# The first pair of images: plain projections ahead of two attentions, position terms by TensorE, and another order of filters and statistics

## The chip, the cores and the metric

The kernel runs on one core of one Trainium2 chip. The metric is the device time of one execution in microseconds, as the median of five runs. A core has TensorE (PE, with its weight load PEld), VectorE (DVE), ScalarE (ACT), GpSimd (POOL) and SyncE (SP). Each engine works through its own list of instructions in order. SP's list holds most loads from HBM, POOL's list most stores, so an instruction of these two that waits also holds the transfers listed behind it.

## The reference

There are 8 images of 512 x 32 x 32 in fp32. Each is normalised over groups of 16 channels, run through one layer, and added to the input:

```python
t = cbs(x, cv1_w, cv1_bn, 0)                 # 1x1 convolution, 512 -> 512, batch norm, silu
ys = [t[:, :C], t[:, C:]]                    # C = 256
for i in range(N):                           # N = 2
    yi = ys[-1]
    z = cbs(yi, m_cv1_w[i], m_cv1_bn[i], 1)  # 3x3 convolution, 256 -> 256
    z = bot_attention(z, m_qkv_w[i], m_rw[i], m_rh[i])
    z = jax.nn.silu(bn_eval(conv2d(z, m_cv2_w[i], 0), m_cv2_bn[i]))
    ys.append(yi + z)
return cbs(jnp.concatenate(ys, axis=1), cv2_w, cv2_bn, 0)
```

The attention has 4 heads of 64 channels over the 1024 pixels of an image. q, k and v are one 1x1 convolution, 256 to 768. The position term r = rw + rh is added to k; it is the same for all images and has one value for each block i.

## The kernel before

**Pairs.** The images go in four pairs, (0,1) to (6,7). Within a pair, block 0 and block 1 follow each other: a 3x3 convolution of both images, then the projection and attention of the first image, then those of the second. While an attention runs, hooks issue the normalisation and cv1 of the next pair and the transformation of filters, and what they don't finish comes between the two attentions. The two attentions of block 0 are called the first and the second attention here.

**The 3x3 convolution** goes by Winograd tiles of 4 x 4 outputs. `tiles_in` transforms the input on VectorE (w_ec, w_rows, w_d, w_ab, v_in), `conv3x3` multiplies on TensorE (c_ps, L588) and transforms back on VectorE (c_t, c_e, c_r, c_k). The filters are transformed on the chip in the first pair, by `make_u(n, oc, k, area)`: n is the block, oc the block of 128 output channels, k that of input channels. It takes three steps over the filter's rows, with two ScalarE operations and six VectorE operations in each (u_new, L391 to L398) and three more VectorE operations (L375 to L381) ahead of two of the steps, and stores the result through POOL (L402). Later uses load it again with SP (u). For (0, 0, k) the result stays on the chip, in `first_units`.

**Buffers.** Tiles with the same tag share slots. Tag "u" is a ring of ten slots of 4 KB a partition in which filters, filter results (u_new), cv1's weights and the projections' weights follow one another. Tag "pt" has six slots, for the attention's exponentials, the position terms read back (r_in), and the convolution's tiles. Tag "t" has four slots of 2 KB, tag "acc" two. A new tile waits for the last use of the one whose slot it takes, a store's landing included.

**The projection**, `project_strassen` (L778), computes q, k and v by one level of Strassen: seven products instead of eight, each of two matmuls of 512 columns (L791) and four of 128 (L797), with copies on ScalarE and some 21 additions on VectorE (L817 to L870). Its weights are seven sums of blocks of the qkv weights, made by `make_sq` with four operations on VectorE (L212 to L215) and stores, and loaded in four pieces (sq). VectorE makes sums of z for it (t_z, `first_sum`, L775).

**The position terms** are made by `make_r` on POOL: a copy, four additions of 128 x 512 (L200) and four stores (L204) for each block. `project_strassen` reads them back (r_in, L813) and adds them to k (kr, L817). For block 0 `make_r(0, ...)` is issued in the start-up; for block 1 `make_r(1, load_r(1))` is issued after the projection of the second image; its load is issued by SP at 279.20 us of the trace.

**The start-up** normalises image 0 in two halves of 256 channels (`group_norm_part`, statistics on VectorE, or on ScalarE with `by_act`), with gmat, a matrix that POOL makes by two selections (L334, L338), to sum over groups. Image 1 (x_second) takes its statistics from ScalarE. Filters (0, 1, k) are made first and stored, (0, 0, k) after them. `make_sq(0, ...)` comes after the convolution's tiles, with the qkv weights in the padded tiles Y2 (the profile's ypad). `keep_y` stores y0 and y1.

**The order** on each engine comes from a list scheduler, with `tc.issue_after` fixing some instructions behind others. Between the two attentions TensorE does: half of cv1 of an image of the next pair, the first image's last head sums (s_ps, L952), the second image's projection, the first image's second 1x1 convolution (m_ps, L1132), and the rest of cv1. In the direct mode of pair 0, cv1 is plain products of 512 columns (L471).

## Time and profile before

| | us |
|---|---|
| median of five runs | 2366.21 |
| lowest, highest | 2361.94, 2370.42 |
| profiled execution | 2360.92 |
| its span in the trace | 2359.3 |
| TensorE busy | 2227.8 (94%) |
| VectorE busy | 1767.1 (75%) |
| ScalarE busy | 1084.2 (46%) |
| POOL busy | 216.3 (9%) |

The granted TensorE clock was 0.985 of full speed over the span. The stages of pair 0, by events in the trace:

| us | event on TensorE |
|---|---|
| 15.88 | cv1 of image 0 starts |
| 54.75 to 82.42 | cv1 of image 1 |
| 82.42 to 136.16 | 3x3 convolution of both images |
| 136.16 to 160.06 | projection of image 0 |
| 163.55 to 228.45 | first attention, first to last product with v |
| 309.47 | first product with v of the second attention |

Busy time of each engine in these stretches, where a stretch of 69.00 us with PE 60.53 means that TensorE had something in work for 60.53 of them (the lines leave out a column each for the number of instructions):

| stretch | PE | DVE | ACT | POOL |
|---|---|---|---|---|
| 0 to 40 | 19.58 | 26.14 | 15.63 | 22.22 |
| 40 to 82 | 41.06 | 39.03 | 28.69 | 17.01 |
| 82 to 110 | 12.20 | 25.56 | 3.48 | 3.36 |
| 110 to 136 | 25.14 | 24.25 | 5.16 | 0.77 |
| 136 to 160 | 20.73 | 15.75 | 10.54 | 0.54 |
| 160 to 229 | 60.53 | 58.91 | 41.62 | 6.65 |
| 229 to 252 | 16.90 | 11.96 | 5.33 | 6.48 |
| 252 to 310 | 46.12 | 33.83 | 21.00 | 16.34 |

In the lists of waits below, a row names the engine and the instruction that waited, after the arrow the instruction that released it, then the total in us, the number of waits, and the longest. In rows in order of time, the columns are the start, the duration, the engine, the line, the operation, the tiles written and read, and in brackets the idle time before and its releaser. One fp32 matmul instruction appears as two records.

### The profile page before, as it was taken

What the parts mean: (1) busy time and instruction counts of PE and PEld (TensorE: products, weight loads), DVE (VectorE), ACT (ScalarE), POOL (GpSimd) and SP (SyncE); (2) the same over time, 40 slices, a digit from 0 to 9 for tenths busy, and PEclk for the clock granted to TensorE, in tenths of its full rate; (3) what the DMA queues carried; (4) which work ended last, traced back from release to release, by engine and by line L of the source; (5) the groups of instructions that cost most, each with busy time, mean ns of one, the idle gap of its engine ahead of it and who ended that gap; (6) DMA issues with size and microseconds to landing.
All of it is one profiled execution on the core that took longest, in us unless ns stands there. A gap on an engine that the chain in (4) does not pass through costs nothing.

```text
span 2359.3 us, 40593 instructions
## 1 busy us (share of the span) xinstructions
PE 2227.8 (94%) x16378; PEld 1083.3 (46%) x16378; DVE 1767.1 (75%) x2669; ACT 1084.2 (46%) x1321; POOL 216.3 (9%) x423
## 2 busy tenths in 40 slices
PE   6798878999999999999999999999999999999997
PEld 2463423734447343744346444473344734373433
DVE  7987587877857878986775868887794777787652
ACT  5245444355323666355522565635532355336532
POOL 5101210000021000000012000000002100000003
PEclk9899989999999999999999999999999999999999
DMA  9632623621257051523147323351225711161105
GB/s 330 228 121 73 229 81 119 243 87 55 59 152 256 25 174 47 181 95 104 33 114 232 108 87 116 95 195 60 65 66 149 247 34 59 50 203 38 55 19 140
DMA packets 133251, 284.58 MB, mean 121 GB/s; under 512 B 34272, under 2 KB 60368, under 8 KB 132032
## 3 DMA queue, kind: packets, MB, share of 16 engines
q1 hardware_dynamic: 105712, 198.14, 26.0%
q0 software_dynamic: 27344, 83.77, 11.6%
q8 instruction: 131, 2.15, 0.4%
q14 instruction: 64, 0.52, 0.1%
HBM read 213.83 MB, written 68.03 MB: 119 GB/s over the span
## 4 chain that ended last, share of the span: by engine, by line
PE 53%; DVE 23%; issue 11%; DMA 7%; ACT 3%; POOL 2%; SPq 0%; DVEq 0%; POOLq 0%; ACTq 0%
PE av_ps L935 15%; PE l_ps L901 15%; PE p_ps L791 6%; DMA c_out<-in_x_dram 4%; PE m_ps L1132 4%; PE x_ps L1252 3%; PE ps L471 3%; PE c L1152 2%; PE pv_ps L797 2%; DVE acc L921 2%; DVE c_e L596 1%; ACT pt L905 1%; DVE c_t L595 1%; DVE c_t L594 1%; PE s_ps L952 1%
## 5 line engine op out<-in xcount | busy, mean ns | idle before, releaser
L905 ACT ACTIVATE pt<-l_ps 128x1024 f32<-128x1024 f32 x512 | 495.8, 1023 | 366.2 <-PE l_ps L901 333.5
L921 DVE TENSOR_TENSOR acc<-acc,pt 128x1024 f32<-128x1024 f32 x384 | 469.9, 1224 | 88.2 <-ACT pt L905 65.7
L901 PE MATMUL l_ps<-q,kr 64*64 64x512 f32 x4096 | 493.8, 596 | 29.1 <-ACT pt L905 16.3
L935 PE MATMUL av_ps<-pt,vT 64*64 64x512 f32 x4096 | 488.9, 594 | 10.7 <-DVE z L943 8.5
L901 PEld LDWEIGHTS l_ps<-q,kr 64*64 64x64 f32 x4096 | 157.5, 134 | 304.2 <-issue 246.9
L935 PEld LDWEIGHTS av_ps<-pt,vT 64*64 64x64 f32 x4096 | 154.9, 133 | 286.9 <-issue 238.9
L588 PE MATMUL c_ps<-v_in,u 128*64 128x128 f32 x4320 | 239.5, 273 | 5.4 <-issue 4.5
L588 PEld LDWEIGHTS c_ps<-v_in,u 128*64 128x64 f32 x4320 | 235.8, 137 | 12.6 <-issue 11.5
L791 PE MATMUL p_ps<-t_z,sq 128*128 128x512 f32 x256 | 124.6, 608 | 14.0 <-DVE c_t L595 9.1
L1132 PE MATMUL m_ps<-z,m_sb 128*128 128x512 f32 x256 | 112.5, 592 | 0.0
L593 ACT COPY c_m<-c_ps 128x512 f32<-128x512 f32 x48 | 28.1, 586 | 171.4 <-PE c_ps L588 112.2
L919 DVE TENSOR_TENSOR acc<-pt 128x1024 f32<-128x1024 f32 x64 | 78.0, 1218 | 30.7 <-ACT pt L905 30.7
L791 PE MATMUL p_ps<-z,sq 128*128 128x512 f32 x192 | 91.7, 604 | 9.6 <-ACT z L445 9.6
L445 ACT ACTIVATE t<-m_ps,bh,sh 128x512 f32<-128x512 f32 x64 | 47.0, 776 | 87.5 <-PE m_ps L1132 86.9
L1202 POOL DMA_DIRECT2D c_out<-in_x_dram x56 | 49.7, 960 | 304.0 <-ACT c_out L445 301.0
L1132 PEld LDWEIGHTS m_ps<-z,m_sb 128*128 128x128 f32 x256 | 48.2, 190 | 58.4 <-issue 54.8
L1007 DVE TENSOR_TENSOR z<-z,rs 128x512 f32<-128x512 f32 x64 | 44.0, 687 | 34.4 <-DMA rs<-r_dram 34.2
L791 PEld LDWEIGHTS p_ps<-t_z,sq 128*128 128x128 f32 x256 | 44.9, 193 | 51.7 <-issue 34.3
L506 POOL MEMSET w_rows<- 128x32 f32 x48 | 7.9, 164 | 646.3 <-PE s_ps L952 381.2
L797 PEld LDWEIGHTS pv_ps<-sq,z 128*128 128x128 f32 x384 | 49.0, 191 | 29.1 <-issue 11.7
L943 DVE TENSOR_TENSOR z<-av_ps,z 128x512 f32<-128x512 f32 x64 | 43.9, 686 | 22.0 <-ACT z L942 22.0
L445 ACT ACTIVATE c_out<-cz,bh,sh 128x512 f32<-128x512 f32 x14 | 16.7, 1298 | 91.9 <-DVE cz L1229 91.9
(299 smaller groups left out, 3189.9 us busy)
## 6 DMA issues: line engine op xcount, KB each, us to landing
u<-u SPq DMA_DIRECT2D x135, 512.0 KB
sq<-sq SPq DMA_DIRECT2D x48, 384.0 KB
r_in<-r SPq DMA_DIRECT2D x32, 512.0 KB
rs<-r_dram SPq DMA_DIRECT2D x120, 128.0 KB
x<-in_x_dram SPq DMA_DIRECT2D x28, 512.0 KB
y_in<-y SPq DMA_DIRECT2D x28, 512.0 KB
c_out<-in_x_dram POOLq DMA_DIRECT2D x56, 256.0 KB, 5.4
out_dram<-c_out POOLq DMA_DIRECT2D x56, 256.0 KB, 3.2
```

The source lines that it names most:

```text
L445: silued[0] = nc.scalar.activation(dst, src, AF.Silu, scale=sh[:, k : k + 1], bias=bh[:, k : k + 1])
L471: last_product[0] = nc.tensor.matmul(ps[:, half, :], w_of(k), rhs_of(k, half), start=(k == begin), stop=(k == end))
L588: nc.tensor.matmul(to[o], us[cp][:, k, row, c, o], rhs, start=(k == 0), stop=(k == NM - 1),)
L791: nc.tensor.matmul(ps[:, o, :], w[:, o, :], rhs, start=not onto, stop=True, skip_group_check=onto)
L797: nc.tensor.matmul(v[:, ts(j, P)], rhs[:, ts(j, P)], w[:, 2, :], start=j == 0 and not onto, stop=True, skip_group_check=True,)
L901: nc.tensor.matmul(ps[kh * HD : (kh + 1) * HD, hd, :], kr[r, c, o : o + HD], q[r, c, ts(half, HALF)], start=True, stop=True,)
L905: last_exp[0] = exp = nc.scalar.activation(pt, ps, AF.Exp, scale=SCALE)
L919: return nc.vector.tensor_tensor(accs[g], pt[0], pt[1], ALU.add)
L921: ins = nc.vector.tensor_tensor(accs[g], accs[g], pt[i], ALU.add)
L935: nc.tensor.matmul(avs[g][hd * HD : (hd + 1) * HD, kh, :], vT[r, j, o : o + HD], pt[i][r, hd, :], start=(j == 0), stop=(j == NJ - 1),)
L1132: nc.tensor.matmul(pss[oc][:, half, :], m2_sb[:, n, k, ts(oc, P)], ao[:, k, ts(half, HALF)], start=(k == 0), stop=(k == NM - 1),)
L1252: nc.tensor.matmul(ps[:, o, :], w[:, c, ts(o, P)], rhs[c], start=(c == 0 and not onto), stop=(c == 1), skip_group_check=onto,)
```

## The change

It concerns pair 0 alone.

1. Both projections of block 0 in pair 0 use a new `project_direct`: 16 matmuls of 512 columns and 16 of 256 with the plain qkv weights, loaded in two pieces of the new kind "qkv". k = ps + r is one VectorE addition of 128 x 1024, q and v are ScalarE copies. The order is qk(0), v, qk(1); `early` stands before v and `middle` after it. `first_sum` and the sums inside the convolution are not used there.
2. The position terms of block 0 come from `make_r_early`: TensorE adds the two broadcast parts by two matmuls with an identity into each half of a PSUM tile, ScalarE copies them out, SP stores them.
3. The position terms of block 1 still come from `make_r` on POOL, but it is issued at the end of the first attention, behind an addition of its sums, with the raw tile in a slot of tag "acc".
4. `make_sq(0, ...)` (block 0, used from pair 1 on) moves from the start-up to pair 0's first attention of block 1, with tiles of its own instead of the padded tiles.
5. The start-up makes filters (0, 0, k) first, kept in `first_units`, and (0, 1, k) after them; the u_new of the latter take tag "pt" in place of the ring. The second half of image 0's statistics goes to ScalarE. `keep_y(1, ...)` comes after the convolution's tiles.

```diff
+    def make_r_early(n, raw):
+        for c in range(NM):
+            nc.scalar.copy(planes(rw_sb[:, n, c : c + 1]), natural(raw[:, c : c + 1]))
+        ident = act.tile([P, P], F32, tag="h", name="ident", bufs=2)
+        make_identity(nc, ident)
+        for c in range(NM):
+            ps = ps_big.tile([P, NH, HALF], F32, tag="big", name="r_ps")
+            for half in range(NH):
+                to = ps[:, half, :].rearrange("p (h w) -> p h w", w=F)
+                nc.tensor.matmul(
+                    to, ident, rw_sb[:, n, c].unsqueeze(1).to_broadcast([P, ROWS, F]), start=True, stop=False
+                )
+                nc.tensor.matmul(
+                    to, ident, rh_sb[:, n, c, ts(half, ROWS)].unsqueeze(2).to_broadcast([P, ROWS, F]),
+                    start=False, stop=True,
+                )
+            for half in range(NH):
+                r = act.tile([P, HALF], F32, tag="t", name="r_new", bufs=4)
+                nc.scalar.copy(r, ps[:, half, :])
+                nc.sync.dma_start(r_dram[n][c][:, ts(half, HALF)], r)
...
+    def u_new_early():
+        return act.tile([P, 2, 2, P], F32, tag="pt", name="u_new", bufs=6)
...
+        def project_direct(n, z, w, early=None, middle=None):
...
+            def qk(c):
+                for which in (1, 0):
+                    o = which * C + c * P
+                    ps = conv1x1(
+                        lambda k: w[k][:, o : o + P], lambda k, half: z[:, k, ts(half, HALF)], NM
+                    )
+                    if which == 0:
+                        nc.scalar.copy(q[:, c], ps.rearrange("p a b -> p (a b)"))
+                    else:
+                        tt(kr[:, c], ps.rearrange("p a b -> p (a b)"), rs[c], ALU.add)
+
+            qk(0)
+            if early:
+                early()
+            per = NH * HALF // C
+            for j0 in range(0, NJ, per):
+                ps = big()
+                for j in range(per):
+                    at, o = divmod(j * C, HALF)
+                    for k in range(NM):
+                        nc.tensor.matmul(
+                            ps[:, at, o : o + C], z[:, k, ts(j0 + j, P)], w[k][:, 2 * C : 3 * C],
+                            start=(k == 0 and o == 0), stop=True, skip_group_check=True,
+                        )
+                nc.scalar.copy(vT[:, j0 : j0 + per, :], ps.rearrange("p a (b o) -> p (a b) o", o=C))
+            if middle:
+                middle()
+            for c in range(1, NM):
+                qk(c)
+            return q, kr, vT, lambda: None
...
-    norm = s.group_norm_part(xs[NX // 2 :])
-    chunk = make_u(0, 1, 0, areas[0, 1, 0])
+    norm = s.group_norm_part(xs[NX // 2 :], by_act=True)
+    chunk = make_u(0, 0, 0, areas[0, 0, 0], first_units)
...
-    make_r(0, rw_raw)
+    make_r_early(0, rw_raw)
+    chunk = make_u(0, 1, 0, areas[0, 1, 0], new=u_new_early)
...
-    with tc.issue_after(last.ins):
-        make_sq(0, tiles, sums)
+        keep_y(1, y0s, Y1[1])
...
-        w = take_blocks("sq", 0, 0, SQ_NAMES)
-        qkv = s.project_strassen(0, z[:, :, 0], w, t)
+        if direct:
+            qkv = s.project_direct(0, z[:, :, 0], [take(key) for key in direct_keys(0)])
...
-            t = s.first_sum(z[:, :, 1])
+            if p == 0:
+                with tc.issue_after(end.added.ins):
+                    make_r(1, load_r(1, "acc", 2))
...
-            if p == 0:
-                make_r(1, load_r(1))
+            if direct:
+                qkv = s.project_direct(
+                    0, z[:, :, 1], [take(key) for key in direct_keys(1)], early=end.sums, middle=middle
+                )
                 feed(cv1_keys(1))
...
+            tiles = [act.tile([P, 3 * C], F32, tag=tag, name="qkv_raw") for tag in ("p3", "p4")]
+            load_qkv(0, tiles)
+            sums = [act.tile([P, 3, P], F32, tag="t", name="sq_new", bufs=4) for _ in range(4)]
+            behind[2] = lambda: make_sq(0, tiles, sums)
```

## The prediction

> **What bounds the kernel now.** I read the page's busy table and its 40 slices first, to see where TensorE is not full; then the list of waits by engine, over 0 to 160 us and 160 to 320 us; then the order in time around each wait named there; last the busy time by stretch.
>
> ```profile
> PE 2227.8 (94%) x16378; PEld 1083.3 (46%) x16378; DVE 1767.1 (75%) x2669; ACT 1084.2 (46%) x1321; POOL 216.3 (9%) x423
> ...
> PE   6798878999999999999999999999999999999997
> ...
> PEclk9899989999999999999999999999999999999999
> ```
>
> TensorE is the bound. Apart from the last, all its slices under 9 lie in the first 413 us (seven of 59 us each), the part that the change rewrites. The waits there, 0 to 160 us first:
>
> ```profile
> PE gm_ps L645 <- POOL gmat L338: 11.3, 1, 11.3
> PE c_ps L588 <- DVE c_t L595: 8.1, 1, 8.1
> PE c_ps L588 <- DVE v_in L543: 7.6, 1, 7.6
> PE gm_ps L645 <- DVE mv L684: 5.3, 1, 5.3
> ...
> PE p_ps L791 <- DVE c_t L595: 1.9, 1, 1.9
> ```
>
> 160 to 320 us:
>
> ```profile
> PE l_ps L901 <- DVE q L854: 10.6, 1, 10.6
> PE p_ps L791 <- ACT y_half L445: 4.9, 1, 4.9
> ...
> PE s_ps L952 <- ACT y_half L445: 1.8, 1, 1.8
> ```
>
> In order of time the 10.6 us has its cause just above it: VectorE held for a store of r, with all of the second image's recombination queued behind.
>
> ```profile
> 294.51 1.04 POOL L200 TENSOR_TENSOR r_new<-rw_sb,rh_sb 128x512 f32<-128x512 f32 x1 [6.40 <-DMA r<-r_new]
> ...
> 298.60 0.69 DVE L536 SCALAR_TENSOR_TENSOR v_new<-w_d 128x512 f32<-128x512 f32 x1 [17.38 <-DMA r<-r_new]
> ...
> 303.91 1.98 PE L901 MATMUL l_ps<-q,kr 64*64 64x512 f32 x8 [10.56 <-DVE q L854]
> ```
>
> The sum is made against the profiled execution, 2360.9 us (span 2359.3); the median of the five runs, 2366.2, is 5.3 above it. A difference under 0.3%, 7.1 us, I count as none.
>
> **Part 1, start to the first attention.** Prices: 32 records of 128x512 took 14.00 us at 228.45, two records to an instruction: 0.87 each (I count 0.86, which misses 0.2 us in a stage); 8 records of 128 columns took 1.05 with their start, 0.22 an instruction; 256 columns, which before has not, are put half way, 0.43.
>
> *Direct products* (16 of 512 columns, 16 of 256) are 16 x 0.86 + 16 x 0.43 = 20.6 us; Strassen's 14 and 28 are 14 x 0.86 + 28 x 0.22 = 18.2. TensorE gets 2.4 us more per image. VectorE loses about 15.7 us of recombination (21 operations of 512 at about 0.69, one of 1.23) for two adds of 1.22; ScalarE goes from 6.2 to 4.1. Weight loads shrink from 1.4 MB to 0.8 MB per image.
>
> *r by TensorE*: eight matmuls, 8 x 0.86 = 6.9 us of PE, and four ScalarE copies (0.59), in place of four POOL adds. They stand between the first image's cv1 and the second's. In before that place has 5.3 us of idle (gm_ps) and the second cv1 starts at 54.75. By hand in the changed order: gmat no longer sits behind a store (3.4 us earlier), ScalarE's statistics of the first image's second half cost 7 us of PE idle, r_ps runs to 51.1, the rest of cv1 to 59.7, second image 59.7 to 87.3: 4.9 later than before (82.4). VectorE covers this, as it ends last.
>
> *Filters* of the second output block now store through a six-slot ring: the fourth set waits for landings that POOL issues only after ScalarE's parts, about 55 us. VectorE, free of waits there before (filters end at 65.4), ends them at 68.9 if a store takes 3.2 us, 71.7 at 5.8 (the output's and the early stores' rows). The second tile stage starts at 76.4 or 79.2, against 75.44.
>
> *Gone from VectorE*: the wait of 2.09 for a memset at 85.75 (it was behind the y_half stores), make_sq's four operations at 107.76 (2.2 in steps), the 1.72 wait for the filter load at 118.31 and the filter's three operations there (1.65), t_z (0.6). With 76.4: tiles done 106.6, conv resumes 107.3 instead of 110.00 and ends at 131 instead of 136.16 (2.7 + 1.72 + part of the rest); the second half of z is ready 137.1 instead of 143.96, silu 0.9 later. The k=0 products are done by then; four of 512 columns, 15 of 256 and qk(1) follow: 138.0 + 3.4 + 6.5 + 6.9 = 154.8 for the first logits (before 160.06), first av 158.3 (before 163.55). So -5.2, or -2.4 with 5.8 us stores; the stores nearest by place and queue take 5 to 6.5, so I take **-4**. Ends: -8, if the ring never waits, and +3, if stores take 11 us (1.08 per us).
>
> **Part 2, first attention.** make_sq moves beside it: 2.2 us on VectorE, which was busy 58.9 of 69 us in 160 to 229. make_r(1) moves to its end; its load lands some 5.4 us after issue (279.20 to 284.62 before), near 224.6, and its four POOL adds (1.05 to 1.2) run beside VectorE's sums. At 25.5 us such an add beside VectorE stretched an operation of 0.42 to 1.27. Four times 0.85 is 3.4 us of VectorE, with 10 us of slack: **+0.5** on PE; ends 0 and +3. POOL's filter store behind them (222.88 before) leaves about 4 us later.
>
> The Trainium skill's page "SBUF: State Buffer", section "Who interferes with whom", speaks against this move: a VectorE instruction with two SBUF inputs and a GpSimd one that reads SBUF exclude each other for a whole instruction. By it the price would be 4 x 1.2 = 4.8 us of VectorE instead of 3.4, and the sum 1.4 us worse even with no slack.
>
> **Part 3, last av of the first attention to first av of the second.** Before: 228.45 to 309.47, 81.0 us. After, keeping 228.45 as the start: cv1's 16 products to 242.3; kr0 and q0 (8 x 0.86) to 249.2. ScalarE's next y_half stands behind a u_new that waits for a store landing near 252.5; s_ps starts at 255.6 (6.4 idle, where before had 1.8 + 4.9). The v products wait for the kr add, which VectorE has behind five filter sets, 260.5 (4.3 idle); v ends 267.4. A filter store issued at 262.5 lands 268.3 with 5.8 us; SP issues a filter load behind it and only then the attention sums' load: three small transfers in a row (1.6 each, by the sums' store and load issued at 219.34 and 220.97 before, and 0.5 of issue each), the reciprocal and the scaling, 7.1 in all, let z's last scaling end at 275.4. Then 15 products (m2's last two, 13 of cv1), 12.9, to 288.3; qk(1) 6.9 to 295.2; first av 3.5 later, 298.7. The 17.4 us at v_new has no successor: r's four stores were issued before 235. That is **-10.8**.
>
> Ends: all waits gone, PE's own work is 28.0 + 20.6 + 6.9 + 0.6 = 56.1, first av at 288.1, -21; upward +3, if the longest wait for a store here before, ScalarE's 13.9 us up to 243.07, comes on top of what I count.
>
> Late next is z's scaling, 275.4: products behind it can't fill in.
>
> **Sum**: -4 + 0.5 - 10.8 = -14.3, so 2346.6 profiled and 2351.9 as a median; I say 2352. Later pairs keep their code and I cost them at nothing: attention's PE rate (3.43 us per step of two) covers it. If the store order shifts there, the row is u_new's waits, 1 to 3 us.
>
> **Rivals.**
> *A: stores throttle both stages, no measurable change.* Part 3 has three store landings in series (y_half's, u_new's, the one ahead of SP's load), part 1 one. Each us beyond 5.8 costs 3 + 1. For: ScalarE waited 13.9 for a u_new store up to 243.07, VectorE 10.9 in four; stores there took 6.0. From 7.6 us the gain falls under 7.1. At 8.5: -14.3 + 4 x 2.7 = -3.5, median 2363.
> *B: slower, by SP's queue.* The filter loads now stand ahead of the sums' load, and VectorE's filters ahead of kr. What holds SP delays m2, cv1, qk(1) one for one. It decides against the change from 21.4 us (14.3 + 7.1): that landing at 290 rather than 268. At 25 us later: +10.7, median 2377. For: in before these loads stood behind the sums. Against: 25 us is four more store landings than I count, and the ring has six of its ten slots free for filters here, against four.
> *C: more gain.* The ring slots not held by Strassen's blocks (two weights an image in place of four) let filters run ahead, and the 10.7 us of idle I left in part 3 goes: -4 - 21 + 0.5 = -24.5, median 2342. Against: VectorE's filter work is the same and the store queue is one.
> *D: the wait at v_new stays*, with r's chain only shifted: 10.6 back, -3.7, median 2362.5. The order of instructions leaves r's stores over 50 us of time, so it gets little.
>
> **How the numbers follow.** Forecast (-8 to -20) 0.52, C 0.16, A 0.16, D 0.03, B and other losses 0.13. The median for -8 to -20 is 2346 to 2358. Out of the range I leave half of C's tail and most of B: 2338 to 2370. Faster by over 0.3% (below 2359.1): forecast, C and a little of A, 0.70. Within: 0.18. Slower: 0.12.
>
> **What would show it.** Right: no r wait at v_new, no l_ps wait on q; first logits near 155, first av of the second attention near 299; the second image's cv1 later (60); VectorE idle on u<-u_new at 53 to 62; TensorE idle twice at 249 to 261. Wrong: z's scaling past 285; tiles ending past 110; first av of the first attention past 163; stretched sums near 225 that hold TensorE.

## The result, and the profile after

The changed kernel took 2363.81 us (median of 24 runs), the kernel before, run beside it, 2364.55 (44 runs). The ratio is 0.9998, with a 95% interval from 0.9993 to 1.0004: no change. Forecast was 2352 with a clear gain. The time lies inside the stated range, but the gain did not come.

The page of the changed kernel, busy times and slices:

```profile
PE 2242.6 (95%) x16354; PEld 1087.4 (46%) x16354; DVE 1742.1 (74%) x2626; ACT 1088.1 (46%) x1325; POOL 210.7 (9%) x416
...
PE   7798799999999999999999999999999999999997
...
PEclk9899999999999999999999999999999999999999
```

VectorE is busy for 25 us less than before (1742.1 against 1767.1), close to the 2 x (15.7 - 2.4) that the forecast counted for the additions of the two Strassen products. TensorE is busy for 14.8 us more. Part of that was forecast (2 x 2.4 for the plain products, 6.9 for r). The sixth and seventh slice have filled up; the first, second, fourth and fifth are still under 9.

The list of TensorE's waits, 0 to 160 us, and below the mark of omission 160 to 320 us:

```profile
PE gm_ps L676 <- DVE mv L670: 8.1, 1, 8.1
PE c_ps L619 <- ACT c_m L624: 7.2, 1, 7.2
PE c_ps L619 <- DVE v_in L574: 5.9, 1, 5.9
PE gv_ps L676 <- DVE dev L688: 5.0, 2, 4.1
...
PE s_ps L1024 <- ACT y_half L476: 4.8, 1, 4.8
PE ps L502 <- ACT y_half L476: 4.5, 1, 4.5
...
PE p_ps L833 <- DVE kr L822: 2.5, 1, 2.5
PE m_ps L1205 <- DVE z L1079: 2.2, 1, 2.2
```

The wait of 11.3 for gmat is gone, and so is the one of 10.6 of l_ps on q. The first became 8.1 for statistics. The second has no successor of that kind: the chain of r is away from v_new, as the row of that operation shows, which before stood at 298.60 with 17.38 us of idle ahead of it and now has none:

```profile
289.75 0.68 DVE L567 SCALAR_TENSOR_TENSOR v_new<-w_d 128x512 f32<-128x512 f32 x1
...
303.85 1.90 PE L1007 MATMUL av_ps<-pt,vT 64*64 64x512 f32 x16
```

So the forecast's largest wait did go, and the first product with v of the second attention came at 303.85, where it was 309.47. The profiled executions by events, in us of their spans, with three versions that are explained below:

| first product with v of | before | forecast | after | r(1) moved alone | after, filter step late | the same, weight loads held |
|---|---|---|---|---|---|---|
| first attention | 163.6 | 159.6 | 161.9 | 162.5 | 158.9 | 159.0 |
| second attention | 309.5 | 295.2 | 303.9 | 301.5 | 300.2 | 297.8 |
| first attention of block 1 | 470.1 | 455.8 | 464.5 | 462.9 | 460.8 | 457.9 |
| second attention of block 1 | 554.8 | 540.5 | 553.8 | 548.2 | 547.0 | 544.3 |
| median against before | | -14.3 | -0.7 | -6.7 | -4.2 | -8.9 |

The forecast's column is before plus its own steps. The kernel after is 5.6 us ahead at the second attention and only 1.0 ahead at the end of the list. Behind 555 us the code is the same, and there the after profile loses another 6 (1810.4 us against 1804.5). The 17 profiles of this case took 1803.7 to 1811.2 us for that code, so these 6 us are scatter. The profiled executions also lie differently against their medians: that of after 1.9 us above, that of before 3.6 below, that of e14 3.8 below. The profiles show places, and the medians decide on the time.

Where the start-up's gain went is one row of VectorE, in order of time, with the load it waits for (SP's queue below the mark):

```profile
53.90 0.56 DVE L406 TENSOR_TENSOR ypad<-ypad 128x384 f32<-128x384 f32 x1 [10.31 <-DMA ypad<-in_m_cv_w_dram]
...
30.73 7.07 SPq L177 DMA_DIRECT2D rh_sb<-in_m_rh_dram  x1
37.91 2.57 SPq L129 DMA_DIRECT2D ypad<-in_m_cv_w_dram  x1
```

The ypad here is the second of block 1's four filters. (The expectations below call it the first. The first one's load was issued at 30.14, and its operations come at 165.31.) Nothing needs it before the stage between the two attentions, where its other operations stand (234 to 245 us), but the scheduler placed three of its operations (L406 to L408) ahead of five of the six steps of block 0's last two filters, and its load stands in SP's queue behind an issue that took 7.07 us. In the kernel before, these operations stood at 118.31 and waited 1.72.

What took the gain between the attentions is what `make_sq` brought there. POOL's queue, then SP's below the mark:

```profile
243.83 0.77 POOL L253 DMA_DIRECT2D sq<-qkv_raw  x1 [5.66 <-DMA qkv_raw<-in_m_qkv_w_dram]
244.60 0.59 POOL L433 DMA_DIRECT2D u<-u_new  x1
245.18 0.75 POOL L253 DMA_DIRECT2D sq<-qkv_raw  x1
...
232.15 1.48 SPq L243 DMA_DIRECT2D qkv_raw<-in_m_qkv_w_dram  x2
```

Three of its results are plain blocks, stored straight from the loaded weights. Their stores stand in POOL's queue among the filter stores, and they wait for the load of 2 x 384 KB that SP issued at 232.15. Until it landed, POOL stood for 5.66 us with filter stores behind it.

### The profile page after: what moved, and what is told of

Its sections match the earlier page's. It is cut to its first block, busy times and chain, and to the rows that moved or that the text cites. A ratio compares the mean times of both kernels' runs of the same rounds, so it can differ in the third digit from the quotient of the medians.

```text
span 2364.2 us, 40480 instructions
## 1 busy us (share of the span) xinstructions
PE 2242.6 (95%) x16354; PEld 1087.4 (46%) x16354; DVE 1742.1 (74%) x2626; ACT 1088.1 (46%) x1325; POOL 210.7 (9%) x416
## 4 chain that ended last, share of the span: by engine, by line
PE 58%; DVE 16%; issue 13%; DMA 4%; ACT 2%; POOL 1%; SPq 0%; DVEq 0%; ACTq 0%; POOLq 0%
PE av_ps L1007 12%; PE l_ps L973 12%; PE c L1225 7%; PE c_new L1225 5%; PE p_ps L863 5%; PE m_ps L1205 4%; PE c_ps L619 3%; PE x_ps L1325 3%; PE ps L502 2%; DVE acc L993 2%; PE pv_ps L869 2%; ACT pt L977 1%; PE s_ps L1024 1%; PE p_ps L869 1%; DMA rs<-r_dram 1%
## 5 line engine op out<-in xcount | busy, mean ns | idle before, releaser
L973 PE MATMUL l_ps<-q,kr 64*64 64x512 f32 x4096 | 491.0, 593 | 16.1 <-ACT pt L977 14.3
L1007 PE MATMUL av_ps<-pt,vT 64*64 64x512 f32 x4096 | 493.3, 599 | 10.8 <-DVE z L1015 8.5
L619 PEld LDWEIGHTS c_ps<-v_in,u 128*64 128x64 f32 x4320 | 235.8, 137 | 14.8 <-issue 14.7
L863 PE MATMUL p_ps<-t_z,sq 128*128 128x512 f32 x224 | 106.7, 597 | 7.9 <-DVE c_t L626 7.9
L863 PE MATMUL p_ps<-z,sq 128*128 128x512 f32 x168 | 80.2, 604 | 8.2 <-ACT z L476 8.2
L1275 POOL DMA_DIRECT2D c_out<-in_x_dram x56 | 50.5, 977 | 309.5 <-ACT c_out L476 306.6
L1205 PEld LDWEIGHTS m_ps<-z,m_sb 128*128 128x128 f32 x256 | 48.2, 190 | 61.0 <-issue 54.5
L476 ACT ACTIVATE z<-z,bh,sh 128x512 f32<-128x512 f32 x64 | 46.9, 804 | 30.6 <-DVE z L657 29.7
L863 PEld LDWEIGHTS p_ps<-t_z,sq 128*128 128x128 f32 x224 | 38.7, 190 | 40.0 <-issue 28.9
```

The lines of the kernel that those rows point to most:

```text
L476: silued[0] = nc.scalar.activation(dst, src, AF.Silu, scale=sh[:, k : k + 1], bias=bh[:, k : k + 1])
L619: nc.tensor.matmul(to[o], us[cp][:, k, row, c, o], rhs, start=(k == 0), stop=(k == NM - 1),)
L863: nc.tensor.matmul(ps[:, o, :], w[:, o, :], rhs, start=not onto, stop=True, skip_group_check=onto)
L973: nc.tensor.matmul(ps[kh * HD : (kh + 1) * HD, hd, :], kr[r, c, o : o + HD], q[r, c, ts(half, HALF)], start=True, stop=True,)
L1007: nc.tensor.matmul(avs[g][hd * HD : (hd + 1) * HD, kh, :], vT[r, j, o : o + HD], pt[i][r, hd, :], start=(j == 0), stop=(j == NJ - 1),)
L1205: nc.tensor.matmul(pss[oc][:, half, :], m2_sb[:, n, k, ts(oc, P)], ao[:, k, ts(half, HALF)], start=(k == 0), stop=(k == NM - 1),)
```

## The experiments

Each is compared with the kernel before, run on the same chip. The times are medians, the interval is that of the ratio, and where two versions are compared below, it is by their differences against before. With 5 runs the interval is some 3 us to either side, with 9 to 12 it is 2 to 2.6, so single differences of 2 us are not resolved.

| version | us | against before | interval of the ratio |
|---|---|---|---|
| e1: before, r(1) moved | 2356.45 | -6.7 | 0.9965 to 0.9987 |
| e6: e1, plain products | 2360.37 | -2.7 | 0.9984 to 1.0001 |
| e7: e1, r(0) by TensorE | 2354.47 | -8.6 | 0.9949 to 0.9974 |
| e9: e1, new order | 2360.24 | -2.8 | 0.9978 to 0.9995 |
| e13: e7, new order | 2355.56 | -8.0 | 0.9949 to 0.9976 |
| e10: e6, weight sums late, loads held | 2359.66 | -3.9 | 0.9972 to 0.9990 |
| e11: e10, r(0) by TensorE | 2354.05 | -9.5 | 0.9948 to 0.9975 |
| e12: e11, loads not held | 2358.57 | -5.0 | 0.9975 to 0.9993 |
| after: e12, new order | 2363.81 | -0.7 | 0.9993 to 1.0004 |
| e3: after, loads held | 2356.00 | -7.2 | 0.9962 to 0.9982 |
| e4: after, sums at a later hook | 2362.67 | -0.5 | 0.9990 to 1.0008 |
| e5: after, block 1's filters loaded late | 2363.37 | +0.2 | 0.9989 to 1.0011 |
| e8: e3 and e5 | 2357.68 | -5.4 | 0.9968 to 0.9986 |
| e14: after, only the three operations late | 2359.83 | -4.2 | 0.9976 to 0.9997 |
| e15: e14, loads held | 2355.15 | -8.9 | 0.9948 to 0.9973 |
| e16: after, statistics by VectorE | 2363.63 | -0.4 | 0.9990 to 1.0015 |

### What the move of r(1) does alone (e1)

The kernel before, with `make_r(1, ...)` at the end of the first attention and nothing else:

```diff
+            if p == 0:
+                with tc.issue_after(end.added.ins):
+                    make_r(1, load_r(1, "acc", 2))
...
-                make_r(1, load_r(1))
```

> The kernel before with part 3 alone: the position terms of block 1 are made at the end of the first attention, all else as before (Strassen products, start-up, order of filters). Theory L (landings of stores set the stage between the two attentions): the wait of 17.4 us at v_new goes, but the filter stores behind POOL's four additions land later, and the stage, 81.0 us from the last product with v to the first of the second attention, shrinks by 5 or less: 2360 to 2363 as a median against 2364.6. Rival V (the wait at v_new alone cost the stage 10.6): the stage shrinks by 9 to 11, median 2354 to 2356. Rival P (TensorE's added work in the plain products ate the gain in the changed kernel): as V, since this kernel has no plain products.

Measured: 2356.45, 6.7 us below before, and in the profile 74.1 us from the last product with v of the first attention to the first of the second, against 81.0. The wait list of 160 to 320 us of this kernel:

```profile
PE s_ps L952 <- ACT y_half L445: 5.3, 1, 5.3
PE p_ps L791 <- ACT y_half L445: 3.9, 1, 3.9
...
PE l_ps L901 <- DVE q L861: 1.3, 1, 1.3
PE l_ps L901 <- DVE q L854: 1.2, 1, 1.2
```

Of the 10.6 us on q 2.5 are left (two waits), and the waits on y_half have grown from 6.7 to 9.2: 8.1 gained, 2.5 given back there. The median lies just above the range of theories V and P, but the stage shrank by 6.9, more than theory L said and less than V and P did. One edit of a few lines is thus worth more than the whole change, and the rest of the change costs 6 us.

### The loads of the weights (e3, e4)

e3 is the kernel after, with the loads of `make_sq(0)` held. A load has no wait of its own to hold it by, so two VectorE memsets of one column, issued behind the second image's m2, write into the tiles first:

```diff
+            with tc.issue_after(last.ins):
+                for t_raw in tiles:
+                    nc.vector.memset(t_raw[:, :1], 0.0)
             load_qkv(0, tiles)
```

> The changed kernel with the loads of the qkv weights for make_sq(0) held until the end of block 0 by a small memset into each tile; in the changed kernel they are loaded at 232 us and three blocks of them stored from 243.8 on, between the two attentions, where DMA was 0.93 busy from 229 to 252. Theory L: with 1.4 MB less to move there, filter stores land in 2.3 to 2.7 us as before instead of 4.3, three landings in a row, so the stage shrinks from 78.0 by 4 to 6, median 2358 to 2360. Rival Q (the chain is set by the order on DVE, ACT and POOL, and not by landing times): the stage stays within 1.5 us of 78.0, median 2362 to 2365.

e4 leaves the loads where they are and puts the four operations at a later hook, behind two pairs of the attention's sums:

```diff
-            behind[2] = lambda: make_sq(0, tiles, sums)
+            behind[2, 2] = lambda: make_sq(0, tiles, sums)
```

> The changed kernel with make_sq(0)'s four VectorE operations two steps later in the first attention of block 1, behind two pairs of its sums in place of ahead of them. Theory D (the four operations stand right behind a wait of 4.9 us for rs and push the sums, so that TensorE waits 2.2 us and its clock falls): that attention takes 57.4 to 58.5 us in place of 61.4, median 2360 to 2361 against 2363.8. Rival S (VectorE has no room for 2.2 us there at any place): it takes 60 or more, median as the changed kernel.

Measured: holding the loads gives 2356.00, 7.2 below before where the kernel after is 0.7 below. Moving the operations gives nothing (2362.67; theory D fails). So the price is that of the transfers, and not of VectorE's 2.2 us. Neither theory of e3 fits as a whole: the gap between the attentions is 76.9 in place of 77.9, which is rival Q's, and the median lies below theory L's. The first attention of block 1 takes 58.2 us in place of 61.4.

The 3.8 us that the first attention of block 1 lost are seen in VectorE's order of time, in the kernel after:

```profile
500.57 0.69 DVE L1079 TENSOR_TENSOR z<-z,rs 128x512 f32<-128x512 f32 x1 [4.88 <-DMA rs<-r_dram]
501.18 0.55 DVE L234 TENSOR_TENSOR sq_new<-qkv_raw 128x384 f32<-128x384 f32 x1
...
503.17 2.55 DVE L993 TENSOR_TENSOR acc<-acc,pt 128x1024 f32<-128x1024 f32 x2
```

The reciprocals (rs) come 4.88 us late, and the four operations of `make_sq` then stand ahead of the sums that have piled up. Before, a wait as long (4.8) was harmless, with nothing put behind it. In the five profiles with the loads not held and the operations at this place (after, e5, e12, e14, e16) the stage took 58.1 to 61.4 us, so the profile of after shows the worst of it, not the rule.

### The loads of block 1's filters (e5, e8)

e5 is the kernel after, with the loads of block 1's filters held until the convolution's tiles are done, again by a memset of a column. The edit was meant for the one filter that VectorE waits for, but it stands in a loop over all four:

```diff
             for oc, k, at in keys:
+                with tc.issue_after(tiles_done.ins):
+                    nc.vector.memset(inside(Y2[at])[:, :1], 0.0)
                 yield from make_u(1, oc, k, load_raw(1, oc, k, Y2[at]))
```

> The changed kernel with the load of block 1's first filter, and so its three VectorE operations, held until the convolution's tiles are done by a small memset; in the changed kernel VectorE waits 10.3 us for that load at 43.6 to 53.9 us. Theory F (that wait delays all later filters and tiles): the filters end at 64 to 67 instead of 70.2, the first attention starts 2 to 5 us earlier, median 2359 to 2362. Rival G (VectorE would wait for the six slots of the filter results at the same place): filters end at 69 to 71, and the operations come back in the convolution with their 1.7 us; median 2363 to 2366.

e8 has this and the held weight loads of e3.

> After, with both holds: the loads of the qkv weights for the sums held until the second image's m2, and the load of block 1's first filter held until the tiles are done. Theory W: two separate losses, so the gains of the profiles add: first av of the first attention about 158.5, the gap between the two attentions about 76, the first attention of block 1 about 58, and the time is 2352 to 2355 (2356.0 less the 3.3 us of the start-up). Rival S (the time won in the start-up is lost again in a later wait, as it was when it was held alone, 2363.37): 2356 to 2358.

Measured: in the profiles the convolution of pair 0 takes 45.4 us (e5) and 46.4 (e8) in place of 49.9, and the first product with v comes at 158.6 and 158.4, 3.3 and 3.4 earlier. The medians do not follow: 2363.37 and 2357.68. VectorE's row in e5 says why part is lost:

```profile
166.68 0.42 DVE L424 TENSOR_TENSOR u_new<-ypad 128x256 f32<-128x256 f32 x1 [4.53 <-DMA ypad<-in_m_cv_w_dram]
```

This is another filter than the one of the 10.3 us. The first filter's load, issued at 30.14 in after, is issued at 162.17 here, behind a memset that VectorE reaches at 162.08, and lands too late for the first attention, which is 1.3 us longer (68.9) in e5, and 3.2 (70.8) in e8. The second filter's load goes at 112.15, and no wait on it is of note. The edit moved two loads that matter, so it can't say what the early wait costs.

### The parts one by one (e6, e7, e9)

All three start from e1 and add one part. e6 takes `project_direct` for both projections:

```diff
-            qkv = s.project_strassen(0, z[:, :, 0], w, t)
+            qkv = s.project_direct(0, z[:, :, 0], [take(key) for key in direct_keys(0)])
```

> Before with the move of r(1) (the version that measured 2356.45) and the plain products of both projections; r(0) stays on POOL, the sums of the qkv weights stay in the start-up, and so does the old order of filters. Theory W (what the change gives back was lost to the loads and stores of the sums of weights and to the early filter load, not to the products): the plain products cost TensorE 2 x 2.4 us and free 21 operations of VectorE per image, so first logits about 157 to 159 in place of 160, the second attention starts no later, and the time is 2353 to 2358. Theory P (the extra 4.8 us of TensorE is what eats the gain): TensorE has little idle left in these stages, the time is 2359 to 2362, and both stretches with a projection are about 2.4 us longer.

e7 takes `make_r_early`:

```diff
-    make_r(0, rw_raw)
+    make_r_early(0, rw_raw)
```

> Before with the move of r(1) (2356.45) and r(0) by TensorE. Theory W: the 6.9 us of TensorE fill the place of the wait on gmat and VectorE ends the tiles last, so the convolution of pair 0 ends within 1 us of 136 and the time is 2355 to 2358. Theory R (the start-up is bound by TensorE, which the r products delay): the second image's cv1 and the convolution start 4 to 7 us later and the time is 2360 to 2363.

e9 takes the new order alone (filters (0, 0, k) first, u_new in tag "pt", statistics by ScalarE, y1 kept later):

```diff
-    chunk = make_u(0, 1, 0, areas[0, 1, 0])
+    norm = s.group_norm_part(xs[NX // 2 :], by_act=True)
+    chunk = make_u(0, 0, 0, areas[0, 0, 0], first_units)
```

> Before with the move of r(1) (2356.45) and the new order alone: filters of the first output block first, the others' results in slots of tag pt, statistics of image 0's second half by ScalarE, y1 kept after the tiles. r(0) by POOL, Strassen products, sums of weights in the start-up. Theory W: the order by itself is worth little either way, since VectorE has the same operations: tiles done within 3 us of before, the time 2354 to 2358. Theory O (the order is what gives the gain back): tiles done at 112 or later, the time 2359 to 2363.

Measured against e1: plain products +4.0 (theory P's time), r by TensorE -1.9, the order +3.9 (theory O's time). So two of the three parts cost when they come alone. For the plain products the profile of e6 shows the place. From the end of the convolution (137.2) to the first logits (162.4) are 25.1 us, against 22.2 in e1. Its PE rows there:

```profile
141.37 1.96 PE L474 MATMUL ps<-z,w_qkv 128*128 128x512 f32 x4 [2.17 <-DVE c_t L598]
143.16 0.59 PE L805 MATMUL p_ps<-w_qkv,z 128*128 128x256 f32 x2
145.39 3.70 PE L474 MATMUL ps<-z,w_qkv 128*128 128x512 f32 x8 [1.63 <-ACT z L448]
148.92 6.64 PE L805 MATMUL p_ps<-w_qkv,z 128*128 128x256 f32 x30
155.40 7.03 PE L474 MATMUL ps<-z,w_qkv 128*128 128x512 f32 x16
```

The last half of z is ready at 145.39, and all that follows is TensorE work in one chain: 17 us to the first logits. Of Strassen's seven products, five are left behind that point in e1, and they take 13.2 us (145.75 to 158.99). What the plain products save is VectorE's time, and here VectorE isn't what is waited for.

### The parts together (e10 to e13)

e10 is e6 with the weight sums out of the start-up and their loads held, e11 adds r by TensorE, e12 is e11 with the loads where the change has them, e13 is e7 with the new order.

```diff
-    with tc.issue_after(last.ins):
-        make_sq(0, tiles, sums)
...
+            load_qkv(0, tiles)
+            sums = [act.tile([P, 3, P], F32, tag="t", name="sq_new", bufs=4) for _ in range(4)]
+            behind[2] = lambda: make_sq(0, tiles, sums)
```

> Before with the move of r(1), the plain products (2360.37 with these two), and the sums of the weights moved to the first attention of block 1, their loads held until the second image's m2. r(0) by POOL, the old order. Theory V (plain products do not pay by themselves; what pays is that they let the sums leave the start-up): VectorE has 2.2 us of sums and their place less in front of the transformation back, first logits 2 to 4 us earlier than the 162.4 of the kernel with plain products alone, gap and first attention of block 1 as there (75.4 and 57.4 to 58.2), the time 2356 to 2358.5. Rival: the sums were covered in the start-up, first logits at 162 again and the time 2359.5 to 2362.

> After without its new order of filters and statistics, and with the loads for the sums held: the move of r(1), r(0) by TensorE, plain products, sums late and loaded late. Theory V: the order costs some 3.8 us here as it did alone (2360.24 against 2356.45), so this is 2352 to 2354 (2356.0 with the order), first av of the first attention 158 to 160. Rival N (the order is needed once r stands on TensorE and the sums have gone; its price alone does not carry over): 2356 to 2359, first av 162 or later.

> The same with the loads for the sums where the change has them, at the end of the first attention. Theory L (these loads and the stores that follow cost 6 to 8 us wherever the order stands): 2359 to 2361.5, the gap 2 to 5 us longer and the first attention of block 1 2 to 4 us longer than in the kernel with the loads held. Rival M (only together with the new order, whose first filter of block 1 is early, do they collide): 2353 to 2356.5, both stretches within 1 us.

> Before with the move of r(1), r(0) by TensorE and the new order; Strassen products, sums of the weights in the start-up. If the prices add (2354.47 with the first two, and 3.8 for the order): 2357.5 to 2359.5, first av of the first attention 163 to 165. If the order suits r on TensorE: 2353 to 2356, first av 160 to 162.

Measured: e10 2359.66, above what theory V gave it and in the rival's range, though its first logits came at 156.4. Moving the sums out of the start-up gained 6 us in the profile there and 0.7 in the median. Part of that is scatter (e6's profile is 3.1 below its median, e10's 0.1 above, and it has the longest time of all behind 555 us), the rest is open. e11 is at 2354.05, below the version with the new order (e3, 2356.00) by 2.3, less than the 3.8 expected and within the intervals. e12 shows the loads' price without the new order: 4.5 us. Its 2358.57 lies between the two theories and nearer to L. It lies in the first attention (+1.3) and in the gap (+1.2). The first attention of block 1, where theory L saw 2 to 4 us, is 58.1 against 58.2. In e13 the time is 1.1 above e7's, and 0.6 by the differences against before, not 3.8: with r on TensorE no price of the order is seen within the intervals. r by TensorE is worth 1.9 (e1 to e7), 5.6 (e10 to e11) and 5.2 (e9 to e13), more than its own forecast, which was that VectorE covers it.

These kernels also show where the early wait of 10.3 us comes from. With the sums of the weights in the start-up (before, e1, e9, e13) they hold the padded tile, and the second filter's load goes at 108 to 114 us, with waits of 1.7 to 1.9. With the sums moved out (e10, e11, e12) it goes at 39 to 43, and its operations stand at 53 to 56 without a wait of note. Only with the new order as well (after, e3, e4, e16) does VectorE stand for it, 10.3 to 13.9 us. So two parts of the change make this wait together.

### The three operations (e14, e15, e16)

The step that e5 could not price: the load stays early, and only the three VectorE operations that waited for it are put behind the tiles. No other instruction of VectorE changes its place in the start-up.

```diff
             for oc, k, at in keys:
-                yield from make_u(1, oc, k, load_raw(1, oc, k, Y2[at]))
+                chunk = make_u(1, oc, k, load_raw(1, oc, k, Y2[at]))
+                for _ in range(3):
+                    with tc.issue_after(tiles_done.ins):
+                        made = next(chunk)
+                    yield made
+                yield from chunk
```

> After, where only the three VectorE operations on block 1's first filter that waited 10.3 us for its load (at 43.6 to 53.9) stand behind the convolution's tiles instead; the load itself stays early. Theory E (this wait is the price of the new order): tiles done near 106, first av near 158.6 (after 161.9), no wait for that load in the first attention, and the time is 2359 to 2361 (after 2363.8). Rival F (the start-up's time is lost again in the first attention, whatever frees it): first av 158.6 to 160, the first attention 1.5 to 3 us longer than 67.6, the time 2362 to 2364.5.

e15 is e14 with the weight loads held as in e3.

> The same with the loads for the sums held until the second image's m2 (2356.0 with this alone). Theory E: 2352 to 2354, which would be the shortest of all. Rival F: 2355 to 2357.5.

e16 is the kernel after with `by_act=True` taken out.

```diff
-    norm = s.group_norm_part(xs[NX // 2 :], by_act=True)
+    norm = s.group_norm_part(xs[NX // 2 :])
```

> After, with the statistics of image 0's second half on VectorE as before. Theory E: the wait for the filter's load stays, VectorE gets four more operations in front of the filters, and the time is 2363 to 2367. Rival G (the price is the 7 us of TensorE's wait on ScalarE's statistics): cv1 of image 0 ends earlier, the convolution starts up to 3 us earlier than 85.5, and the time is 2359 to 2362.

Measured: e14 is at 2359.83, e15 at 2355.15, e16 at 2363.63 (its wait for the filter's load has grown to 13.9). Theory E holds for e14, with the first product with v at 158.9 and the first attention not longer (65.7). e15 is 1.15 above theory E's range and at the lower end of rival F's, and its interval of 3 us can't part the two; its first attention (66.5) isn't longer either. By these, the three operations cost 3.5 us in the kernel after, and 1.7 with the loads held (e3 to e15). VectorE's waits in e14, 0 to 137 us:

```profile
DVE taps L410 <- ACT u_new L423: 7.4, 1, 7.4
DVE st L669 <- DMA x<-in_x_dram: 4.8, 1, 4.8
```

Of the 10.3 us that went, 7.4 came back as a wait for ScalarE. VectorE is 3.15 us earlier from there on (the tiles start at 67.01 against 70.16).

e15 against e14 is a third price for the weight loads: 4.7. The views of the transfers from the end of the first attention, 59 us each, first e14, then e15 below the mark (instruction, engine, count, KB each, median us from issue to landing):

```profile
DMA packets 7210, 14.65 MB, mean 248 GB/s; under 512 B 1172, under 2 KB 3480, under 8 KB 7208
u<-u_new POOLq DMA_DIRECT2D x19, 256.0 KB, 5.0
qkv_raw<-in_m_qkv_w_dram SPq DMA_DIRECT2D x2, 384.0 KB
sq<-qkv_raw POOLq DMA_DIRECT2D x3, 192.0 KB, 4.9
...
DMA packets 6731, 13.29 MB, mean 225 GB/s; under 512 B 1092, under 2 KB 3400, under 8 KB 6728
u<-u_new POOLq DMA_DIRECT2D x19, 256.0 KB, 4.0
```

With 1.36 MB less in this stretch (the two loads and the three stores are 1344 KB, 1.38 MB), a filter store lands after 4.0 us in place of 5.0, and z's scaling comes at 273.65 in place of 275.54. That the slower stores are what costs is argued and not shown: in e12 and e11 a store lands after 4.1 and 4.2 us, and the loads still cost 4.5. Nor is the loss at one place: in after against e3 most of it is in the first attention of block 1 (3.2), in e14 against e15 in the gap (79.0 against 75.8), in e12 against e11 in the first attention and the gap. Common to the three early versions is POOL's wait for the weights' load (5.66 in after, 4.51 in e14, 6.66 in e12) with filter stores behind it.

**The account, by medians against before:** r(1) moved -6.7; r by TensorE -1.9 more; plain products with the sums late and held -0.9 more (e11, -9.5); the new order without the three operations +0.6 (e15, -8.9); the weight loads early +4.7 (e14, -4.2); the three operations early +3.5 (after, -0.7). The steps of -1.9, -0.9 and +0.6 are inside the scatter. The price of the loads stands on three pairs of kernels (4.5, 4.7 and 6.5); by which path it arises is in part open. That of the three operations stands on two (3.5 and 1.7) whose intervals still touch, and on their profiles, which part by 3.0 us at the first attention.

Four versions beat both kernels by 0.4%: e7, e11, e13 and e15 (0.9961, 0.9962, 0.9963 and 0.9961). The simplest is e7: the kernel before, with r(1) moved and r(0) by TensorE, and with neither the plain products nor the new order.

## Why the prediction was wrong, point by point

**Part 1, start to the first attention: -4 forecast, -1.7 in the profile of after, -4.6 in e14.** The step that failed is the one on the filters: it had VectorE ending them at 68.9 to 71.7, held up by store landings alone. They ended at 70.16, which looks right and is luck. In after VectorE waits for such a store for 0.3 us from 60 to 112 us, and instead a load that the step did not consider held it for 10.3 us. The terms behind the filters were too short as well. With the 1.2 us that the forecast allowed for stores, the second tile stage was to start at 77.6 and did (77.64), but the tiles were done at 109.2 in place of 107.8, the last half of z came at 141.4 in place of 139.2, and the first logits at 158.4 in place of 156.0. With the three operations out of the way the filters end at 67.0, earlier than the forecast's best, and the stages behind them are as long as in after. So that e14's -4.6 lies near the forecast's -4 is in part two errors that cancel. Two smaller terms hold: from the last half of z to the first logits 17.0 us (forecast 16.8), 16 products of 256 columns at 0.44 each (taken as 0.43).

**Part 2, the first attention: +0.5 forecast, -0.9 in the profile (67.6 against 68.5, from the first logits to the last product with v).** The price of r's additions beside VectorE was about right. Rows of POOL, then of VectorE below the mark:

```profile
215.12 3.37 POOL L222 TENSOR_TENSOR r_new<-rw_sb,rh_sb 128x512 f32<-128x512 f32 x2
221.08 2.06 POOL L222 TENSOR_TENSOR r_new<-rw_sb,rh_sb 128x512 f32<-128x512 f32 x2
...
216.05 1.53 DVE L1079 TENSOR_TENSOR z<-z,rs 128x512 f32<-128x512 f32 x1
217.51 1.26 DVE L424 TENSOR_TENSOR u_new<-ypad 128x256 f32<-128x256 f32 x1
219.61 4.62 DVE L993 TENSOR_TENSOR acc<-acc,pt 128x1024 f32<-128x1024 f32 x2
```

Against 0.69, 0.42 and 2.55 for the same operations alone, VectorE lost 0.84 + 0.84 + 2.07 = 3.75 us, and it had the slack. Forecast was 3.4. The Trainium skill's page "SBUF — State Buffer", section "Who interferes with whom", says that a VectorE instruction with two SBUF inputs contends with a GpSimd one that reads SBUF, and that one locks the other out. The prediction's estimate by that page was 4.8; the measured loss lies between.

The step that failed here is "make_sq moves beside it: 2.2 us on VectorE". It named the wrong attention (the operations come in the first attention of block 1), and it priced only the operations. It left out 1344 KB of loads and stores that the move brings to the end of the first attention and into POOL's and SP's queues there. They cost 4.5 to 6.5 us. This is the largest loss of the change, and the forecast had it at zero.

**Part 3, between the attentions: -10.8 forecast, -3.1 in the profile of after, -6.9 for the move alone.** That the wait at v_new would go, and have no successor, was right, and so were the last 23 us (end of z's scaling to the first product with v: 23.3 forecast, 23.5 measured). The term that failed is z's scaling. Its end was forecast 46.95 us behind the last product with v of the first attention and came 54.5 behind it (280.37), 7.5 late. Of that, 3.3 is the chain of small transfers: forecast 7.1 from the issue of the sums' load, it took 10.4. The rows of VectorE:

```profile
274.53 0.20 DVE L1067 RECIPROCAL rc<-sums_all 128x8 f32<-128x8 f32 x1 [10.20 <-DMA sums_all<-s_dram]
279.68 0.69 DVE L1079 TENSOR_TENSOR z<-z,rs 128x512 f32<-128x512 f32 x1 [4.94 <-DMA rs<-r_dram]
```

The load of 4 KB issued at 269.92 took 4.6 us to its reciprocal, where 2.1 with its issue were counted, by a pair of such transfers at 219 to 221 us of the kernel before. There the DMA engines were 0.02 busy, and from 269 to 275 us of after 0.79. In three other profiles this load took 2.4 (before), 3.7 (e15) and 3.9 (e14). The spread behind it, a store and two loads of 128 KB, took another 4.9, with the DMA engines 0.17 busy, and as long with the weight loads held (e3, e15), so traffic does not explain that part. The other 4.2 is that SP got to the sums' load later, behind waits on y_half of 9.3 (4.5 and 4.8) in place of 6.4, and behind the filter load. With the weight loads held (e15) the scaling ended 52.3 behind: 2.2 of the 7.5 are theirs, and 5.4 were mis-sized without them.

Without the loads' price and the early wait (e15) the gain is 8.9 of the forecast's 14.3. The profile of e15 is 2.6 behind the forecast at the second attention (297.8 against 295.2); where the rest of the 5.4 went stays open.

**"Later pairs cost nothing"** holds from 555 us on within the scatter. Pair 0's own first attention of block 1, which has the sums now, was no later pair and was left out of the sum.

**The rivals.** A named the measured time (2363 by stores that throttle), but not its cause: it needed filter stores of 7.6 us and more, and their median in after was 5.1, less than the 5.8 that the forecast itself had taken. B did not come: SP was past the filter load ahead of the sums at 268, not at 290. C's size came from no side. D did not come, since v_new has no wait.

## What to carry to other kernels

When work is moved, price its transfers and the queue they enter first, and its instructions last: here 2.2 us of VectorE were harmless, and 1344 KB beside it cost some 5 us. Look through the list of instructions after the move for one that waits on a load and has been pulled ahead of urgent work; three operations of 1.7 us in all cost 3.5 (1.7 in a second pair of kernels). And a small transfer's time should be taken from a row with as much traffic as it will meet: 2.1 us counted became 4.6 here.

## What was not expected of the hardware

A hole in TensorE's work cost more than its length. In the convolution's first products, after a wait of 5.87 us for v_in, 64 records took 5.95 us (kernel after), and after one of 2.64 us 3.71 (e14):

```profile
96.83 5.95 PE L619 MATMUL c_ps<-v_in,u_new 128*64 128x128 f32 x64 [5.87 <-DVE v_in L574]
...
93.32 3.71 PE L619 MATMUL c_ps<-v_in,u_new 128*64 128x128 f32 x64 [2.64 <-DVE v_in L574]
```

Likewise eight records of 512 columns took 5.40 us after the hole of 4.53 in front of q, and 3.60 without one. The granted clock of the profile goes with it: 0.50 from 95 to 101 us in after, 1.00 from 93 to 97 in e14. The forecast counted the two holes between the attentions with their length alone.

How long a hole must be is not the same at the two places. In front of q, the eight records took 3.70 us behind waits of 3.10 to 3.57 (e6, e8, e10) and 5.10 to 6.75 behind waits of 3.75 to 5.81 (nine profiles). The convolution's 64 records took 3.71 behind waits of 2.0 to 2.6 (e5, e8, e13, e14), but 5.38 behind 2.0 to 2.8 (e7, e11, e12, e15), with a granted clock of 0.50 from 95 to 98 us in e11. So a hole of 2 us cost 1.7 us in some kernels and nothing in others, and what decides is open.

The Trainium skill's page "TensorE: Matmul & The Clock Gate", section "Part 1: The HAM clock gate", puts the clock at half after at least one idle window of about 3.4 us. The rows of q agree with that; the convolution's rows behind holes of 2 us do not, and there the measurement decides.

r by TensorE was worth 2 to 6 us, though it put 6.9 us of products into the start-up. In e1 POOL's four additions for it stand at 24.6 to 37.5 us. Six operations of VectorE in that time took 6.6 us, and the same ones 1.8 in e7, where the additions are gone; from there VectorE runs some 5 us ahead (a step of the statistics at 43.23 in place of 48.27). At the start of the tiles it then waits 5.3 us for ScalarE, and the first product with v comes 0.8 earlier (161.7 against 162.5). That the additions are the whole of the gain was not tried apart.
